# Folding the last 64 channels into a copy of the first 128: two statistics passes instead of three

## The chip, the cores and the metric

One core of one Trainium2 chip. The time is the device time of one execution in microseconds (us); medians of several runs are quoted. All runs here were in the fast state (granted clock 0.989 to 0.994 of full speed in every profiled run). A ratio is the mean time of one kernel's fast runs over that of the other's of the same rounds, so it isn't quite the ratio of the medians beside it.

Engine names in the profile: PE is TensorE's matmul, PEld its weight load, DVE is VectorE, ACT is ScalarE, POOL is GpSimd, SP issues transfers. The names that the lines use most: `st` is the PSUM bank of the statistics, `x` the activations, `sq` their squares, `dev` the variance computed from `st`, `dv` its inverse root spread over partitions by transfers, `yn` the normalised input of the MLP, `ph` and `hid` the MLP's first product and its gelu, `sc` the attention scores, `win` the scaled input of the attention, `vbd` the attention's values, `y` a piece of the convolution. A bank is one of the blocks of PSUM into which TensorE writes its products.

## The reference, cut to what matters

A shifted-window transformer block on 16 images of 192 channels and 56x56 pixels, then a convolution whose weights depend on the image. What the change touches are the two layer norms over the channels:

```python
def _ln(x, g, b, eps=1e-05):
    mu = x.mean(-1, keepdims=True)                  # over 192 channels
    var = ((x - mu) ** 2).mean(-1, keepdims=True)
    return (x - mu) / jnp.sqrt(var + eps) * g + b
h = _ln(transpose(x), norm1_g, norm1_b)             # before the attention
# ... window attention; x1 = shortcut + projection
y = _ln(transpose(x1), norm2_g, norm2_b)            # before the MLP
```

## The kernel before

The work goes in 64 steps of 7 rows of an image in each half (392 pixels a half, `T`). Channels lie on partitions: `x0` holds channels 0 to 127 for both halves, `x1` holds channels 128 to 191, the first half of the image on partitions 0 to 63, the second on 64 to 127. The sums over channels, which cross partitions, are made on TensorE with a constant matrix `sel` of 1/192, 32 columns wide. Each half and each of the two norms ("side") has its own 32 rows of the output, so four such matmuls fill the array side by side.

```python
def norm_squares(key, i, side, engine, ...):
    # squares of x0 and x1 (ACT or GpSimd), then on GpSimd:
    for h in range(2):
        p = slice(h * 64, h * 64 + 64)
        nc.gpsimd.tensor_tensor(s0[p, h], s0[p, h], s1[p], ALU.add)   # line 263
    sqs[key] = s0

def norm_stats(keys, steps):
    for side in keys:
        stats[side] = bank(side)
    for k in range(3):                       # three passes
        for side in keys:
            v0, v1 = flat_of(steps[side])
            for h in range(2):
                p = (side if k < 2 else 1 - side) * 64 + h * 32
                dst = stats[side][p : p + 32, :T]
                if k == 0:   mm(dst, sel[:, 0], v0[:, h], True, False)
                elif k == 1: mm(dst, sel[:, 1 + h], v1, False, True)
                else:        mm(dst, sel[:, 0], sqs[keys[side]][:, h], True, True)
    ...

def norm_vars(keys, tag="dev"):              # mean squared on ACT, then on VectorE:
    ...
    nc.vector.tensor_tensor(d[var[s]], stats[s][var[s], :T], d[var[s]], ALU.subtract)
```

One step of the loop, cut. `A, B_, C, D` are the four pairs of PSUM banks:

```python
for i in range(2, NS + 2):
    A, B_, C, D = pairs
    cs = conv_ready(...)                     # up to two pieces of the convolution
    ...
    norm1_scale(i + 1, dvs.pop(0), nc.vector)
    def after():                             # first tap on ACT, three more on VectorE
        ys.extend(conv_begin(*c) for c in cs[1:])
        for c, y in zip(cs, ys):
            conv_rest(*c, y)
    def between():
        singles[0] = banks(f"st_{i}", C)     # the statistics take bank pair C
        keys.update(stats_of(i))
        if keys:
            var.append(norm_vars(keys))
    mlp_first(i - 2, yns.pop(i - 2), hid, (A, B_, C, D, A, B_), after, between)
    # mlp_first: ph 0..2, gelu 0..2, after(), half of ph 3..5, between(), the rest, gelu 3..5
    top, share = attention_scores(i, *qs.pop(i), (C, D, A, B_))   # first scores: pair C
    # ... softmax, next q/k, spread of 1/sqrt(var) by transfers (dv)
    # ... mlp_wide, yn = x * dv and squares on GpSimd, attention, projection, residual
    pairs = [C, B_, D, A]
```

## Time and profile before

| kernel before | |
|---|---|
| median (first three runs) | 3168.89 us, 3168.42 to 3170.85 |
| PE, DVE, ACT, POOL busy | 99%, 67%, 59%, 31% |
| plain step of the loop | 47.68 us |
| every fourth step (an image's taps are made) | 48.77 us |
| statistics in a step: x passes, sq pass | 1.34 us + 0.77 us |

The busy share says how much of the span an engine executed something. A step is measured from the first statistics matmul to that of the next step, in the list of TensorE's instructions in order of time; since the loop is regular to about 0.01 us in all runs but e6 (a few single steps aside), it is a far finer measure than the total. The lines themselves are in the prediction.

### The profile page before, as it was taken

The page shows a single profiled execution, that of the slowest core. Times are in us where ns is not written, and L with a number is a line of the kernel's source. Part 1 is how long each engine was busy: PE and PEld are TensorE (multiplying, and loading weights), DVE is VectorE, ACT ScalarE, POOL GpSimd, SP SyncE. Part 2 cuts the span into 40 slices and gives each one's busy share as a digit, 9 for nine tenths or more (in the row PEclk, how much of TensorE's full clock was granted, in tenths as well). Part 3 has the DMA queues.
Part 4 walks back from the last instruction along what each step waited for, and adds up shares of the span by engine and source line. Part 5 has one row for each costly group of instructions (what it writes and reads, how often), then busy time and mean ns, then how long its engine had stood idle before and what let it go on. Part 6 is the DMA issues. An engine that isn't in the chain of part 4 may idle for free.

```text
span 3168.7 us, 64205 instructions
## 1 busy us (share of the span) xinstructions
PE 3123.1 (99%) x26162; PEld 1932.8 (61%) x26162; DVE 2126.2 (67%) x3909; ACT 1882.5 (59%) x2990; POOL 975.3 (31%) x882
## 2 busy tenths in 40 slices
PE   8899999999999999999999999999999999999998
PEld 5566566666666666666666666666666666666654
DVE  6645766866766766766767667667667667667664
ACT  3555655656656656556556556556566566566553
POOL 4333233232232332332332332332332332323321
PEclk7999999999999999999999999999999999999999
DMA  4001021111101112011120201211111120111101
GB/s 111 12 21 52 27 63 31 32 57 36 58 27 40 54 32 64 30 52 36 38 57 29 65 26 32 61 32 57 33 43 44 37 62 27 52 39 34 27 27 51
DMA packets 79155, 135.37 MB, mean 43 GB/s; under 512 B 21782, under 2 KB 61468, under 8 KB 76940
## 3 DMA queue, kind: packets, MB, share of 16 engines
q1 hardware_dynamic: 77186, 128.92, 14.0%
q8 instruction: 207, 3.39, 0.5%
q0 software_dynamic: 1168, 1.54, 0.3%
q10 hardware_dynamic: 506, 0.79, 0.1%
q14 instruction: 88, 0.72, 0.1%
HBM read 41.26 MB, written 38.54 MB: 25 GB/s over the span
## 4 chain that ended last, share of the span: by engine, by line
PE 93%; DVE 4%; ACT 3%; issue 0%; DMA 0%; POOL 0%; ACTq 0%; SPq 0%; POOLq 0%; DVEq 0%
PE pf L92 24%; PE ph L92 22%; PE pp L92 8%; PE pv L92 7%; PE po L92 6%; PE pq L92 5%; PE pt L519 5%; PE sc L92 4%; PE st L92 4%; PE pk L92 4%; PE pe L92 4%; DVE vbd L462 1%; DVE x L595 1%; ACT vbd L462 1%; ACT hid L609 0%
## 5 line engine op out<-in xcount | busy, mean ns | idle before, releaser
L92 PE MATMUL ph<-yn,wf 128*128 128x392 f32 (+1 forms) x3072 | 806.2, 499 | 3.8 <-ACT hid L609 3.2
L92 PE MATMUL pf<-hid,wf 128*128 128x392 f32 (+1 forms) x3072 | 802.8, 494 | 3.5 <-ACT hid L609 2.0
L506 POOL TENSOR_TENSOR prob<-e,tot 113x588 f32<-113x588 f32 x256 | 298.2, 1176 | 1189.8 <-DVE tot L505 1168.1
L92 PEld LDWEIGHTS ph<-yn,wf 128*128 128x128 f32 (+1 forms) x3072 | 422.5, 188 | 359.1 <-issue 78.9
L462 ACT COPY vbd<-pv 49x192 f32<-49x192 f32 x512 | 160.5, 314 | 696.2 <-DVE vbd L462 691.6
L92 PEld LDWEIGHTS pf<-hid,wf 128*128 128x128 f32 (+1 forms) x3072 | 386.3, 164 | 303.7 <-issue 120.0
L655 DVE SCALAR_TENSOR_TENSOR x<-pf,cols,x 128x784 f32<-128x784 f32 (+1 forms) x128 | 106.1, 829 | 528.5 <-PE pf L92 485.9
L609 ACT ACTIVATE hid<-ph,f1b 128x784 f32<-128x784 f32 x384 | 337.1, 913 | 100.8 <-PE ph L92 99.4
L263 POOL TENSOR_TENSOR sq<-sq,sq 64x392 f32<-64x392 f32 x252 | 260.4, 1033 | 372.2 <-ACT sq L257 357.9
L718 DVE SCALAR_TENSOR_TENSOR y<-x,wt,y 128x770 f32<-128x770 f32 x282 | 321.1, 1148 | 16.8 <-ACT y L711 8.3
L358 POOL TENSOR_TENSOR yn<-x,dv 128x784 f32<-128x784 f32 x62 | 115.2, 1858 | 534.5 <-DMA dv<-dev 534.5
L92 PEld LDWEIGHTS pv<-wqkv,win 64*128 64x128 f32 (+1 forms) x2048 | 255.7, 189 | 31.5 <-issue 1.2
L92 PE MATMUL pv<-wqkv,win 64*128 64x192 f32 (+1 forms) x2048 | 272.8, 326 | 0.5 <-ACT kbd L416 0.5
L497 DVE TENSOR_TENSOR e<-e,top 113x588 f32<-113x588 f32 x256 | 267.0, 1043 | 8.9
L490 DVE TENSOR_TENSOR e<-sc,bias_t 113x588 f32<-113x588 f32 x256 | 179.4, 763 | 123.8 <-PE sc L92 123.8
L92 PE MATMUL pp<-o,wp 128*128 128x392 f32 (+2 forms) x896 | 251.4, 514 | 0.0
L245 ACT ACT_TABLE_LOAD x193 | 247.6, 1283 | 5.2 <-issue 1.8
L525 ACT COPY prt<-pt 128x678 f32<-128x678 f32 x256 | 179.3, 727 | 116.5 <-PE pt L519 115.1
L500 ACT ACTIVATE e<-e 113x588 f32<-113x588 f32 x256 | 176.8, 691 | 110.0 <-DVE e L497 109.9
L519 PEld LDWEIGHTS pt<-ident,prob 113*128 113x128 f32 x1536 | 166.8, 142 | 72.3 <-issue 39.9
L92 PE MATMUL po<-prt,vbd 128*64 128x49 f32 x6144 | 199.2, 225 | 4.3 <-ACT kbd L416 4.3
L462 DVE COPY vbd<-pv 49x192 f32<-49x192 f32 x512 | 181.2, 354 | 31.9 <-PE pv L92 24.7
(166 smaller groups left out, 3994.8 us busy)
## 6 DMA issues: line engine op xcount, KB each, us to landing
dv<-dev SPq DMA_DIRECT2D x1012, 49.0 KB
x<-in_x_dram SPq DMA_DIRECT2D x15, 1484.0 KB
out_dram<-y SPq DMA_DIRECT2D x48, 392.0 KB
out_dram<-y SPq DMA_DIRECT2D x48, 196.0 KB
x<-in_x_dram SPq DMA_DIRECT2D x16, 392.0 KB
x<-in_x_dram SPq DMA_DIRECT2D x15, 350.0 KB
out_dram<-y SPq DMA_DIRECT2D x16, 308.0 KB
out_dram<-y SPq DMA_DIRECT2D x16, 154.0 KB
```

The costliest lines, as they stand in the source:

```text
L92: nc.tensor.matmul(dst, lhs, rhs, start=start, stop=stop, skip_group_check=True)
L245: nc.scalar.activation(junk, eps_t[0:1], func)
L263: (adder or nc.gpsimd).tensor_tensor(s0[p, h], s0[p, h], s1[p], ALU.add)
L462: copy(dst, src[s * 64 : s * 64 + N, h, :, :, j, :])
L490: nc.vector.tensor_tensor(e, sc[:PW, :, : HEADS * N], rel, ALU.add)
L497: nc.vector.tensor_tensor(ehs[wp], ehs[wp], t.broadcast_to([PW, 2 * HEADS, N]), ALU.subtract)
L500: nc.scalar.activation(es[wp], es[wp], AF.Exp)
L506: nc.gpsimd.tensor_tensor(prob[wp][:PW, :, 0:N], ehs[wp], t.broadcast_to([PW, 2 * HEADS, N]), ALU.mult)
L519: nc.tensor.transpose(pt[:, a, g * PW : (g + 1) * PW], prob[wp][:PW, h : h + 2, :].rearrange("p h k -> p (h k)"), ident[:PW, :PW],)
L525: nc.scalar.copy(prt, pt[:, :, : 3 * PW])
L609: nc.scalar.activation(hid[:, f], phs[f][:, :, :T], AF.Gelu, bias=f1b[:, f : f + 1])
L718: nc.vector.scalar_tensor_tensor(dst, src, wt[:, kc, t : t + 1], dst, ALU.mult, ALU.add)
```

## The change

The intent is to save TensorE a pass. GpSimd, which is idle two thirds of the time, adds the 64 channels of `x1` onto the matching half of `x0`, the result in a new tile `xs`; transfers copy the half that gets nothing added. The matmul over `xs` then gives the whole mean in one pass. To find room for the adds, they and the squares of step i+3 go ahead of `yn` in GpSimd's order.

```diff
+    def norm_sums(key, i, side):
+        v0, v1 = flat_of(i)
+        s0 = one.tile([128, 2, T], F32, tag=("xs", "o")[side], name=f"xs_{key}")
+        nc.sync.dma_start(s0[64:128, 0], v0[64:128, 0])
+        nc.sync.dma_start(s0[0:64, 1], v0[0:64, 1])
+        for h in range(2):
+            p = slice(h * 64, h * 64 + 64)
+            nc.gpsimd.tensor_tensor(s0[p, h], v0[p, h], v1[p], ALU.add)
+        xss[key] = s0
@@ norm_stats
-        for k in range(3):
+        folded = all(k in xss for k in keys.values())
+        for k in (0, 2) if folded else range(3):
...
-                    if k == 0:
+                    if k == 0 and folded:
+                        mm(dst, sel[:, 0], xss[keys[side]][:, h], True, True)
+                    elif k == 0:
@@ the loop (ahead of it the same sums are added for its first steps)
+        if has(i + 3):
+            norm_sums(f"1_{i + 3}", i + 3, 0)
+            norm_squares(f"1_{i + 3}", i + 3, 0, nc.gpsimd)
         if 1 in keys:
             yns[i - 1] = norm2_scale(i - 1, dvs.pop(1), i == NS)
-        if has(i + 3):
-            norm_squares(f"1_{i + 3}", i + 3, 0, nc.gpsimd)
...
             residual(i, pp, pair1, at)
+            norm_sums(f"2_{i}", i, 1)
```

More of the change, by code (lines that the diff above doesn't have):

```diff
@@ L239, in flat_of @@
         return v0.rearrange("p h r c -> p h (r c)"), v1.rearrange("p r c -> p (r c)")
-    sqs, stats = {}, {}
+    sqs, xss, stats = {}, {}, {}
     def table(func):
@@ L284, in norm_stats @@
             sqs.pop(keys[side])
+            xss.pop(keys[side], None)
     def norm_vars(keys, tag="dev"):
@@ L1030, in tile_swin_then_dynamic_conv @@
     attention_v_out(pvs)
+    norm_sums("1_4", 4, 0)
     yns[0] = norm2_scale(0, dvs.pop(1), True)
@@ L1037, in tile_swin_then_dynamic_conv @@
     residual(1, pp, pair1)
+    norm_sums("2_1", 1, 1)
     norm_squares("2_1", 1, 1, nc.scalar)
```

## The prediction

> **What bounds the kernel now.** I read the page first (busy time, slices, chain), then the list of all waits, then one step of the loop in order of time on every engine, then stretches of exactly one step. The page and the chain:
>
> ```profile
> PE 3123.1 (99%) x26162; PEld 1932.8 (61%) x26162; DVE 2126.2 (67%) x3909; ACT 1882.5 (59%) x2990; POOL 975.3 (31%) x882
> PE 93%; DVE 4%; ACT 3%; issue 0%; DMA 0%; POOL 0%; ACTq 0%; SPq 0%; POOLq 0%; DVEq 0%
> ```
>
> TensorE is busy 99% of the span and is 93% of the chain that ended last. "Busy" alone proves little, so I looked at whether TensorE ever waits. In the list of waits no row of PE itself is over 10 us in the whole run, and one step, from the first statistics matmul to the next, takes 47.67 us with TensorE busy for all of it:
>
> ```profile
> 901.17:948.85 47.68, 47.68 (x409) 29.68 (x407) 32.84 (x61) 29.01 (x47) 14.84 (x13) 1.00 0.09 26
> 1140.66:1188.33 47.67, 47.67 (x408) 29.66 (x406) 33.84 (x60) 29.76 (x48) 14.86 (x13) 1.00 0.11 35
> 1236.01:1284.79 48.78, 48.55 (x413) 29.91 (x411) 31.15 (x63) 28.84 (x46) 15.05 (x13) 1.00 0.17 43
> ```
>
> (Columns: length, then busy us of PE, PEld, DVE, ACT, POOL, granted clock, DMA share, GB/s.) The third row is the step after which an image's filter taps are made, one in four; there TensorE gives up 0.23 us to ACT. So a matmul taken out of the loop is worth its slot, as long as nothing else stands within that distance behind it. The statistics slot, in order of time on TensorE:
>
> ```profile
> 1524.26 1.52 PE L92 MATMUL st<-x,sel 128*32 128x392 f32 x16
> 1525.60 0.84 PE L92 MATMUL st<-sq,sel 128*32 128x392 f32 x8
> 1526.37 4.22 PE L92 MATMUL ph<-yn,wf 128*128 128x392 f32 x12
> ```
>
> The 16 instructions on x are two passes (first 128 channels, then last 64) of four logical matmuls, two instructions each; the 8 on sq are the third. Start to start, two passes take 1525.60 - 1524.26 = 1.34 us, so one takes 0.67 us, and the third took 0.77 to the next product.
>
> **What the Trainium skill says.** "TensorE: Matmul & The Clock Gate", Part 3 (the mechanism): matmuls 32 columns wide in different column tiles run at the same time. The trace agrees: eight such instructions take 0.67 us, while twelve of full width take 1526.37 to 1530.52, 0.35 us each. So the removed eight must not be priced at eight times 0.35 (2.8 us a step), and even less at their listed 498 ns. "SBUF — State Buffer", Who interferes with whom: a VectorE instruction with two SBUF inputs contends with a GpSimd one that reads SBUF; one with at most one SBUF input, outside the two-port modes, does not. The trace agrees: a two-input SBUF product of 64x21 elements, median 0.19 us, took up to 1.33 us beside a GpSimd add, while PSUM copies of L462 stay within 338 to 361 ns and residual adds from PSUM (L595) at 604 at most. "DMA: Bandwidth & Descriptors", Latency and other measured facts: a transfer has a fixed cost of about 2 us; here the spreads landed about 2.1 us after issue (below).
>
> **The change part by part.**
>
> *Removed:* the middle pass, in 63 of the loop's steps (60 with both sides, 3 with one; the three statistics rounds before the loop are not folded). The built programs agree: the statistics stand at the same place in TensorE's order, one pass shorter. The estimate is 63 x 0.67 = 42 us. Of the last three steps part is not bound by TensorE, so I count 41 to 42.
>
> *Added on GpSimd:* four adds of 64x392 a step. The same form costs 1033 ns (L263), so 4.1 us a step, 123 x 2 x 1.03 = 254 us in all: POOL goes from 975 to about 1230 us, 39%. Whether they lie on a path depends on where they stand:
>
> ```profile
> 1507.17 1.86 POOL L358 TENSOR_TENSOR yn<-x,dv 128x784 f32<-128x784 f32 x1 [8.46 <-DMA dv<-dev]
> 1508.99 2.10 POOL L362 TENSOR_TENSOR yn<-x,dv 64x392 f32<-64x392 f32 x2
> 1511.16 1.49 POOL L259 TENSOR_TENSOR sq<-x 128x784 f32<-128x784 f32 x1
> 1512.62 0.84 POOL L260 TENSOR_TENSOR sq<-x 128x392 f32<-128x392 f32 x1
> 1513.53 2.10 POOL L263 TENSOR_TENSOR sq<-sq,sq 64x392 f32<-64x392 f32 x2
> 1520.69 2.10 POOL L263 TENSOR_TENSOR sq<-sq,sq 64x392 f32<-64x392 f32 x2 [5.06 <-ACT sq L257]
> ```
>
> The change puts the sums and squares of step i+3 ahead of yn, into the hole of 8.4 us in which GpSimd waits for the spread. The last softmax product ends 1546.38; sums 2.1, squares 1.49 + 0.84 + 2.10 give about 1553.0. The spread lets yn start at 1554.75 in that step, so yn is late by nothing, with 1.7 us left; and yn ends its first part at 1556.6 while its reader, the first ph, starts at 1563.74. This holds only if the adds don't wait for the copies. They don't: the copies fill the half of the partitions that the adds leave alone, and the built program shows the adds waiting for TensorE (the buffer's previous reader) and older transfers, not for their own. The second pair follows the residual: 1515.1 to 1517.2, in the hole before the squares of ACT at 1520.69, which keep their place. VectorE then copies from PSUM, which does not contend; its two-input products start at 1517.97, after it.
>
> *Added transfers:* four a step, 98 KB each, on the SP queue:
>
> ```profile
> 1547.31 10.54 SPq L312 DMA_DIRECT2D dv<-dev  x16
> 1573.70 0.34 SPq L740 DMA_DIRECT2D out_dram<-y  x1
> ```
>
> Sixteen spreads issue in 10.54 us (0.66 each), the eighth at about 1552.6, and its reader starts at 1554.75: 2.1 us to landing. The first two copies go behind the spreads, 1557.9 to 1559.2, landing about 1561; the second two after the residual (1515.1), issued by 1516.5, landing about 1519, with a wide allowance for 98 KB by 1520. The statistics start at 1524.26. Some 24 MB more on 135 MB at 43 GB/s loads nothing. Where an image is loaded, the queue now holds the load back some 5 us until the residual is done; that load took about 6 us and is read about 25 us later.
>
> *Moved:* after the removed pass, everything up to the next step must come 0.67 us earlier. VectorE is the nearest: before it evicts the scores it idles for 1.22 to 2.6 us waiting for TensorE:
>
> ```profile
> 1193.11 1.14 DVE L295 TENSOR_TENSOR dev<-st,dev 64x392 f32<-64x392 f32 x2
> 1195.47 2.80 DVE L490 TENSOR_TENSOR e<-sc,bias_t 113x588 f32<-113x588 f32 x4 [1.22 <-PE sc L92]
> ```
>
> That is the tightest kind of step and leaves 0.55 us. ACT's wait for the statistics is 1.57 us there or more. Before the statistics ACT (third gelu, ends 1524.10) has almost no slack against TensorE (1524.26), but that stretch is not shortened, so no wait forms. The sum: 3168.9 - 42 = 3127 us.
>
> **The rivals.**
> (1) *GpSimd or the copies become the wait:* the adds wait for their transfers after all, and yn stands behind them. Then yn would start around 1567.7 and end its first part near 1569.6, some 6 us after TensorE wants it, 62 times: about +345 us, near 3500. For it: the order sums, squares, yn. Against it: the regions are disjoint and the built program has no such wait.
> (2) *Contention:* GpSimd's sums slow VectorE. If a third of a microsecond a step reached ACT's vbd copies (they follow VectorE's, and end in the gelu with 0.16 us of slack), 0.2 to 0.3 us a step would come back, 15 to 20 us: about 3143. Against it: PSUM readers show no slowing beside GpSimd.
> (3) *The pass was partly hidden:* if the 0.67 us only overlapped other work, TensorE would be no faster: 3165. Against it: PE is busy throughout and the next product follows at once.
> (4) *More waits on TensorE's queue:* the statistics now wait for four transfers as well as GpSimd and ACT. If each cost 0.05 us visibly, 12 us: 3139. Against it: steps whose statistics already wait for loaded images show the same 1.34 us.
>
> **Range and chances.** I hold the plain sum at some 75%; (2) and (4) together some 17%, which sets the upper end; (3) a few per cent; (1) 2%. Below the sum there is little: only one pass per step can go, so 3118 is already three times the uncertainty of the 0.67 us. Predicted 3127 us, range 3119 to 3142. Faster by over 2% would be under 3105.5, that is 63 us from a 42 us removal: 0.02. Slower by 2%: 0.03. Within 2%: 0.95, so a real gain of 1.3% that the 2% line calls the same.
>
> **What would show it.** Right: the steps are 47.0 us long instead of 47.67; 492 fewer statistics instructions on x; the xs matmuls start about 0.67 us ahead of sq; POOL near 1230 us; yn still released by the dv transfer with an idle time near 1.7 us instead of 8.4; VectorE's idle time before the score eviction 0.55 to 1.9 us; PE still 99%. Wrong: PE rows in the list of waits released by POOL yn, POOL xs or DMA xs; L462 or L342 longer; gaps before st or before the first ph.

## The result, and the profile after

The changed kernel takes 3141.32 us (3138.62 to 3141.79, 4 runs) against 3168.65 us of the kernel before beside it: ratio 0.9911, 95% interval 0.9894 to 0.9929. That is inside the range, and 14 us above the point of 3127 us: some 27 of the 42 us came.

The page of the changed kernel, busy times and the chain that ended last:

```profile
PE 3086.4 (98%) x25670; PEld 1931.8 (62%) x25670; DVE 2126.6 (68%) x3909; ACT 1881.5 (60%) x2990; POOL 1219.2 (39%) x1128
PE 84%; DVE 10%; ACT 2%; issue 2%; DMA 1%; POOL 0%; ACTq 0%; SPq 0%; DVEq 0%; POOLq 0%
```

492 TensorE instructions are gone as forecast, and POOL stands at 1219 us (about 1230 were forecast). But TensorE's part of the chain fell from 93 to 84%, and VectorE's rose from 4 to 10%. GpSimd's part is still 0%, so the adds did not become the bound. GpSimd in one step, in order of time, fits the plan:

```profile
1151.11 2.10 POOL L274 TENSOR_TENSOR xs<-x,x 64x392 f32<-64x392 f32 x2
1153.29 1.49 POOL L259 TENSOR_TENSOR sq<-x 128x784 f32<-128x784 f32 x1
1154.74 0.84 POOL L260 TENSOR_TENSOR sq<-x 128x392 f32<-128x392 f32 x1
1155.66 2.09 POOL L263 TENSOR_TENSOR sq<-sq,sq 64x392 f32<-64x392 f32 x2
1159.34 1.85 POOL L373 TENSOR_TENSOR yn<-x,dv 128x784 f32<-128x784 f32 x1 [1.59 <-DMA dv<-dev]
```

The sums and squares run in the hole, and yn still waits for its transfer, 1.59 us in this step, where the prediction had 1.7; over the loop it is 1.4 to 3.6 us, median 2.1 (8 us and more in the last three steps, which have no sums ahead of it).

Four steps in a row, as stretches (length, then busy us of PE, PEld, DVE, ACT, POOL, clock, DMA share, GB/s):

```profile
939.29:986.60 47.31, 47.17 (x400) 29.67 (x399) 33.89 (x60) 29.76 (x48) 18.82 (x17) 1.00 0.15 44
986.60:1034.13 47.53, 47.17 (x400) 29.67 (x398) 34.08 (x61) 29.58 (x47) 18.87 (x17) 1.00 0.26 77
1034.13:1082.32 48.19, 47.96 (x404) 29.88 (x403) 31.18 (x63) 28.82 (x46) 19.01 (x17) 1.00 0.20 51
1082.32:1129.47 47.15, 47.15 (x400) 29.77 (x398) 32.83 (x61) 28.99 (x47) 18.82 (x17) 1.00 0.13 36
```

Forecast were 47.0 us and 48.1 us. The first steps of the loop, which have no convolution yet, are 47.02 us long in this trace; those with it are not. One step of the second kind, TensorE and VectorE in order of time:

```profile
1176.79 0.94 PE L92 MATMUL st<-xs,sel 128*32 128x392 f32 x8
1177.47 0.92 PE L92 MATMUL st<-sq,sel 128*32 128x392 f32 x8
1177.52 4.07 DVE L733 SCALAR_TENSOR_TENSOR y<-x,wt,y 128x770 f32<-128x770 f32 x4
1178.32 4.22 PE L92 MATMUL ph<-yn,wf 128*128 128x392 f32 x12
1181.62 1.14 DVE L310 TENSOR_TENSOR dev<-st,dev 64x392 f32<-64x392 f32 x2
1182.91 2.24 PE L92 MATMUL sc<-kbd,q 64*64 64x98 f32 x96 [0.37 <-DVE dev L310]
```

There is a wait that did not exist before: the score matmuls (sc) start 0.15 us after VectorE's subtraction (dev) ends at 1182.76, and the profile names it. The first scores go to bank pair C, in which the statistics lie, and dev is their last reader. In the kernel before, the like step had dev end at 1193.11 + 1.14 = 1194.25 and the scores start thus (the window of the view ends inside them), behind the same four taps of the convolution:

```profile
1189.02 4.06 DVE L718 SCALAR_TENSOR_TENSOR y<-x,wt,y 128x770 f32<-128x770 f32 x4
1194.59 1.65 PE L92 MATMUL sc<-kbd,q 64*64 64x98 f32 x67
```

So 0.34 us lay between dev and the scores, and the change needed 0.67. Of the 0.34, the 0.15 us that pass between dev's end and a score matmul that waits for it can't be used. Why dev doesn't come earlier with TensorE: from the residual's second set of adds on, the timeline lists no wait of VectorE before dev (waits over 0.15 us are listed). dev starts 15.4 us after these adds start in both kernels (1177.74 to 1193.11, and 1166.19 to 1181.62), while TensorE's way to the scores became a pass shorter. A second, smaller thing: from the first statistics matmul to the next product it takes 1178.32 - 1176.79 = 1.53 us here, where 2.11 - 0.67 = 1.44 follows from the prediction, and 1.59 in the step after the taps; only the early steps have 1.45.

The medians by kind of step (14 rounds of four, from the traces; a: first after the taps, b and c: two pieces of the convolution, d: the taps are made at its end), for all kernels of this study. The ratios are to the kernel before in the same rounds, whose medians were 3168.4 to 3169.8 us. In e6 the b and c steps vary, from 48.2 to 51.4 us:

| kernel | a | b | c | d | time, us | ratio to before |
|---|---|---|---|---|---|---|
| before | 47.68 | 47.68 | 47.68 | 48.77 | 3168.65 | 1 |
| after | 47.15 | 47.31 | 47.53 | 48.19 | 3141.32 | 0.9911 |
| e1 pass dropped, nothing added | 47.02 | 47.24 | 47.46 | 48.11 | 3137.81 | 0.9898 |
| e2 banks exchanged | 47.16 | 47.09 | 47.10 | 48.19 | 3131.91 | 0.9879 |
| e3 sq pass first | 47.02 | 47.30 | 47.53 | 48.11 | 3137.50 | 0.9898 |
| e4 both | 47.02 | 47.02 | 47.02 | 48.11 | 3126.84 | 0.9864 |
| e5 before, banks exchanged | 47.67 | 47.68 | 47.68 | 48.77 | 3168.49 | 0.9998 |
| e6 yn first on GpSimd | 47.34 | 48.72 | 49.06 | 48.59 | 3197.43 | 1.0092 |
| e7 no adds on GpSimd | 47.02 | 47.30 | 47.53 | 48.11 | 3138.71 | 0.9906 |
| e8 all added, three passes kept | 47.68 | 47.68 | 47.68 | 48.77 | 3168.79 | 0.9999 |
| e9 dev earlier on VectorE | 47.15 | 47.10 | 47.10 | 48.19 | 3132.19 | 0.9886 |
| e10 e4 and the taps' products later | 47.02 | 47.02 | 47.02 | 47.46 | 3115.77 | 0.9834 |

Against 47.02 and 48.11 the changed kernel loses 0.13, 0.29, 0.51 and 0.08 us: 1.01 us in four steps, with 14 such rounds about 14 us, which is the missing time (3141.3 against e4's 3126.8).

### The profile page after: what moved, and what is told of

It is laid out like the page before. It is cut to its first block, busy times and chain, and to the rows that moved or that the text cites. A ratio compares the mean times of both kernels' runs of the same rounds, so it can differ in the third digit from the quotient of the medians.

```text
span 3139.3 us, 64443 instructions
## 1 busy us (share of the span) xinstructions
PE 3086.4 (98%) x25670; PEld 1931.8 (62%) x25670; DVE 2126.6 (68%) x3909; ACT 1881.5 (60%) x2990; POOL 1219.2 (39%) x1128
## 4 chain that ended last, share of the span: by engine, by line
PE 84%; DVE 10%; ACT 2%; issue 2%; DMA 1%; POOL 0%; ACTq 0%; SPq 0%; DVEq 0%; POOLq 0%
PE pf L92 24%; PE ph L92 16%; PE pp L92 8%; PE po L92 6%; PE pv L92 5%; PE pq L92 5%; PE pt L534 5%; PE sc L92 4%; PE pk L92 4%; PE pe L92 4%; DVE y L733 3%; PE st L92 2%; DVE vbd L477 2%; DVE x L610 1%; DVE win L357 1%
## 5 line engine op out<-in xcount | busy, mean ns | idle before, releaser
L477 ACT COPY vbd<-pv 49x192 f32<-49x192 f32 x512 | 160.1, 313 | 693.3 <-DVE vbd L477 688.7
L274 POOL TENSOR_TENSOR xs<-x,x 64x392 f32<-64x392 f32 x246 | 248.9, 1012 | 234.9 <-DVE x L610 225.6
```

The lines of the kernel that those rows point to most:

```text
L274: nc.gpsimd.tensor_tensor(s0[p, h], v0[p, h], v1[p], ALU.add)
L477: copy(dst, src[s * 64 : s * 64 + N, h, :, :, j, :])
```

## The experiments

Three theories for the missing 14 us: the removal runs into dev and its PSUM bank (1); the added adds, transfers or waits cost it (2); the waits in TensorE's queue pull the statistics' four column tiles apart (3, a part of 2). A fourth asks whether the new order on GpSimd matters.

### e1: only the removal

```diff
-        for k in range(3):
+        for k in (0, 2) if drop else range(3):      # drop=True in the loop
```

> The kernel before with the middle statistics pass left out of the loop and nothing added (wrong on purpose: the last 64 channels are missing from the mean). Theory 1 (the removal itself runs into VectorE: the score matmuls reuse the PSUM bank of the statistics, which VectorE's subtraction into dev frees, and in the steps with two pieces of the convolution that comes late): most of the missing 14 us is missing here too, about 3138 us (3168.7 - 42 + 12), steps of 47.0, 47.2-47.3, 47.5 and 48.1 us. Theory 2 (the added adds, transfers and waits cost the 14 us): the full gain, about 3127 us, steps of 47.0 throughout and 48.1 in one of four.

Measured 3137.81 us (ratio 0.9898, 0.9882 to 0.9915). The result still passed the comparison, though it is wrong on purpose: the mean enters only as its square in the variance. The kernel adds nothing at all, and steps b and c are still 0.22 and 0.44 us too long, while a and d are at their floor. One of them, in order of time:

```profile
1180.40 1.14 DVE L295 TENSOR_TENSOR dev<-st,dev 64x392 f32<-64x392 f32 x2
1181.68 1.55 PE L92 MATMUL sc<-kbd,q 64*64 64x98 f32 x62 [0.37 <-DVE dev L295]
```

The same wait of 0.37 us stands in a kernel without any of the added work. Theory 1 holds for steps b and c, and the sizes fit: in the kernel before, the medians from dev's end to the first scores are 0.58 us in b and 0.35 in c; less the 0.15 that a waiting score matmul keeps, 0.43 and 0.20 could be given up, and a pass of 0.66 leaves 0.23 and 0.46. What a and d lose in the changed kernel is absent here, so that part belongs to what was added.

### e2: the banks exchanged

```diff
         mlp_first(i - 2, yns.pop(i - 2), hid, (A, B_, C, D, A, B_), after, between)
+        C, D = D, C
```

> The changed kernel with the banks C and D exchanged after the first MLP half, so that the first scores go to a bank that a gelu freed long ago and only the second quarter of the scores needs the statistics' bank, 0.55 us later. Theory 1: the wait for dev goes, 0.22 and 0.43 us in two steps of four, some 9.6 us: about 3131.5 us; what is left above 3127 is the staggered start of the statistics. Theory 2: no change, 3141 us.

Measured 3131.91 us (0.9879, 0.9864 to 0.9894). Steps b and c fall to 47.09 and 47.10 us; a and d stay at 47.16 and 48.19. The wait for dev is gone from the list of waits. In step c the scores now start before dev has ended (1178.88 + 1.14 = 1180.02):

```profile
1178.88 1.14 DVE L310 TENSOR_TENSOR dev<-st,dev 64x392 f32<-64x392 f32 x2
1179.73 2.24 PE L92 MATMUL sc<-kbd,q 64*64 64x98 f32 x96
```

The change costs no instruction: it only gives the first scores a bank that was freed earlier.

### e3 and e4: the sq pass first, and both

```diff
-        for k in (0, 2) if folded else range(3):
+        for k in (2, 0) if folded else range(3):
```

> The changed kernel with the pass over sq put before the pass over xs, so that TensorE's queue works off the waits for the four transfers while sq streams. Theory 3 (the extra waits in TensorE's queue start the four column tiles up to 0.14 us apart in steps where ACT frees the bank last): the statistics slot goes back from 1.53-1.59 us to 1.44-1.45 us in the convolution's steps, but where dev sets the scores nothing is won, so 3 us: about 3138 us. If the stagger has another cause: 3141 us and slots as before.

> Both edits. If theories 1 and 3 together are the whole loss, the plain sum of the prediction is reached: 3126 to 3128 us, steps of 47.02 us and 48.1 us in one of four. If something else holds it, above 3130 us.

e3 measured 3137.50 us (0.9898, 0.9883 to 0.9913): the slot is back at 1.45 us, a and d reach the floor of 47.02 and 48.11, b and c don't move, because there dev is what the scores wait for. e4 measured 3126.84 us (0.9864, 0.9849 to 0.9878), all four kinds of steps at the floor:

```profile
936.28:983.30 47.02, 47.02 (x400) 29.41 (x398) 33.88 (x60) 29.76 (x48) 18.81 (x17) 1.00 0.15 44
983.30:1030.32 47.02, 47.02 (x400) 29.42 (x398) 34.05 (x61) 29.58 (x47) 18.85 (x17) 1.00 0.26 78
1030.32:1078.44 48.12, 47.89 (x405) 29.66 (x403) 31.17 (x63) 28.83 (x46) 19.01 (x17) 1.00 0.21 51
```

How the queue does it can be read from the single records of the changed kernel's trace in a step of kind a (start in us, duration in ns; the first matmul of each of the four tiles and the wait instructions, the weight loads cut):

```
1082.268  51 Tensor EVENT_SEMAPHORE
1082.320 517 TensorMatrix MATMUL  st<-xs
1082.326 517 TensorMatrix MATMUL  st<-xs
1082.375 489 TensorMatrix MATMUL  st<-xs
1082.393  51 Tensor EVENT_SEMAPHORE
1082.500 489 TensorMatrix MATMUL  st<-xs
```

Here a tile whose data come by two semaphores has a wait instruction of 51 ns of its own ahead of it; the one at 1082.393 stands ahead of the last tile, whose weight load waits for GpSimd besides. In the early steps these waits are worked off while TensorE still streams the product before, and the four tiles start within 0.02 us of each other. Where ACT frees the statistics' bank last, the queue stands in front of them, works them off afterwards, and the fourth tile starts 0.18 us after the first (0.12 in steps b, c and d); the next pass inherits the offset, and the slot is 0.08 to 0.14 us longer. With the sq pass first, these wait instructions are gone from between the tiles, and the four tiles start within 0.02 us in all steps (e3, e4). How the queue works the waits off is read from these records; that the order of the passes removes the loss is what e3 shows.

### e5: the exchange without the change

> Control: the kernel before with the banks C and D exchanged in the same way, three passes kept. Theory 1: there dev is done before the scores want the bank (some 0.35 us or more to spare), so nothing changes: 3168 to 3169 us. If the exchange were worth something by itself (about 9 us), 3159 us, and the gain of the exchange in the changed kernel would not show the wait.

Measured 3168.49 us over 12 runs (0.9998, 0.9989 to 1.0007), with steps of the same length to 0.01 us. The exchange gains nothing by itself. Its gain in e2 is the wait.

### e6: GpSimd's old order

```diff
         if 1 in keys:
             yns[i - 1] = norm2_scale(i - 1, dvs.pop(1), i == NS)
+        if has(i + 3):
+            norm_sums(f"1_{i + 3}", i + 3, 0)
+            norm_squares(f"1_{i + 3}", i + 3, 0, nc.gpsimd)
```

> The changed kernel with GpSimd's old order: yn first, then the sums and squares of step i+3. Theory 4 (the sums are free only because they moved into the hole ahead of yn): the second pair of sums then starts about 2.5 us later, beside VectorE's two-input products, which wait for it; dev comes 1 to 2 us later in the steps with two pieces of the convolution, and the scores with it: 3170 to 3200 us. If GpSimd's order doesn't matter: 3141 us.

Measured 3197.43 us (1.0092, 1.0076 to 1.0107): 28 us slower than before, 56 slower than the change. In one step, GpSimd and VectorE in order of time:

```profile
1143.32 2.26 POOL L274 TENSOR_TENSOR xs<-x,x 64x392 f32<-64x392 f32 x2
1143.58 2.37 DVE L349 TENSOR_TENSOR win<-x,dv 128x343 f32<-128x343 f32 x2
1155.83 1.14 DVE L310 TENSOR_TENSOR dev<-st,dev 64x392 f32<-64x392 f32 x2
1157.11 2.24 PE L92 MATMUL sc<-kbd,q 64*64 64x98 f32 x96 [1.30 <-DVE dev L310]
```

and the same two products in the changed kernel, with the PSUM copies ahead of them, which overlap GpSimd's sums (1167.12 to 1169.21):

```profile
1167.52 2.94 DVE L477 COPY vbd<-pv 49x192 f32<-49x192 f32 x8
1170.50 0.95 DVE L349 TENSOR_TENSOR win<-x,dv 128x343 f32<-128x343 f32 x2
```

The products with two SBUF inputs take 2.37 us beside GpSimd's sums and 0.95 us without. The copies from PSUM take 2.94 us in the changed kernel beside the sums, as in the kernel before. The lost time goes on to dev and from there to the scores, whose wait grows to 1.30 us. A part of the loss is another: the statistics slot grows to 1.72 to 1.78 us, with the fourth tile 0.31 to 0.35 us behind the first, which e6 doesn't separate. So the reordering is not decoration: without it the four adds a step cost more than the removed pass gains.

### e7: no adds

```diff
-        nc.sync.dma_start(s0[64:128, 0], v0[64:128, 0])
-        nc.sync.dma_start(s0[0:64, 1], v0[0:64, 1])
-        for h in range(2): ... nc.gpsimd.tensor_tensor(s0[p, h], v0[p, h], v1[p], ALU.add)
+        nc.sync.dma_start(s0[:, 0], v0[:, 0])
+        nc.sync.dma_start(s0[:, 1], v0[:, 1])
```

> The changed kernel without GpSimd's sums: two transfers of 128 partitions copy both halves (wrong on purpose). Prediction and theories 1 and 3: the adds are off the path, 3139 to 3142 us, the same waits for dev. If the adds slow VectorE or hold yn, up to 14 us faster, 3127 us.

Measured 3138.71 us (0.9906, 0.9889 to 0.9922; wrong on purpose, passed the comparison for the reason given at e1). Steps b and c are the changed kernel's; the adds cost VectorE and yn nothing. The one thing that changes, a little below what was expected, is that a and d come to the floor: without the adds the pass over xs waits for GpSimd no more, so its matmuls have one semaphore less, and the slot is back at 1.45 us. That fits theory 3. So the adds are free as work, but the wait for them isn't: it is part of the 0.13 and 0.08 us of steps a and d.

### e8: everything added, nothing removed

```diff
-        folded = all(k in xss for k in keys.values())
+        folded = False
```

> All the added work (sums, transfers, GpSimd's new order), but the statistics read x in three passes as before; xs is made and not read. Prediction: added work alone costs nothing, 3167 to 3171 us. If it costs what the removal lost: about 3183 us.

Measured 3168.79 us over 12 runs (0.9999, 0.999 to 1.0007). 249 us of GpSimd work (246 adds of 1012 ns) and 25 MB of transfers (160.1 MB against 135.4) are hidden completely. This run can't show what waiting for xs costs, since no matmul reads it, nor whether the work would still be hidden in a step a pass shorter; e7 and e4 show the latter.

### e9: dev earlier on VectorE

```diff
     def between():
         ...
             if keys:
                 var.append(norm_vars(keys))        # dev
+            for c, y in zip(cs[1:], ys[1:]):
+                conv_rest(*c, y, (1,))             # last tap and store of the second piece
```

> The changed kernel with VectorE's subtraction into dev moved ahead of the last tap of the second convolution piece (1.02 us earlier on VectorE), banks as they were. Theory 1: the scores no longer wait for dev, as with the exchanged banks, so the same 9.6 us come back: about 3131.5 us, steps of 47.1 us where they were 47.3 and 47.5. If the bank mattered for another reason than dev's lateness: 3141 us.

Measured 3132.19 us (0.9886, 0.987 to 0.9903), the steps of e2 to 0.01 us. The wait goes in either way: by another bank for the scores, or by an earlier dev, the bank's last reader.

### e10: a better kernel

With e4 the three plain steps are TensorE's own length; the fourth is still 1.09 us longer. In the traces VectorE's residual starts there only after the tap products on TensorE (in the kernel before it waits 4.46 us where a plain step has 2.96).

```diff
             def at():                              # called after the residual's first adds
+                taps(b, pooled, pt)
-                convs[-1]["tt"] = taps_hidden(b, pt)
 ...
         residual(i, pp, pair1, at)
+        if pt is not None:
+            convs[-1]["tt"] = taps_hidden(b, pt)
```

> Exchanged banks and sq first, and in the one step of four that makes an image's taps the residual's first adds are written ahead of the tap products, so that they can't wait for those, and the taps' own add goes behind the residual. If the 1.1 us by which that step is longer come from VectorE waiting for the tap products (it starts the residual 1.5 us later there), 15 steps give up to 1.1 us each: 3110 to 3118 us. If not: 3127 us.

Measured 3115.77 us (0.9834, 0.9819 to 0.9848): 1.7% faster than before, the best here. The fourth step falls to 47.46 us. VectorE's residual now waits 2.76 us there instead of 4.46. Of the remaining 0.44 us, the tap products themselves are the larger part: from their start to that of the next product it takes 0.38 us. What makes the rest was not tested. By the measured step lengths, e4 is the prediction's sum and e10 an addition of another kind.

## Why the prediction was right or wrong

- *What bounds the kernel:* right. TensorE sets the time, and a pass taken away is worth 0.66 us a step where nothing follows close (47.02 against 47.68, early steps and e4).
- *The size of the pass:* right. 63 x 0.67 = 42 us gave 3127; e4, which removes both new waits, measured 3126.84.
- *The added adds:* right as work. e8 shows them free, e7 that dropping them doesn't touch steps b and c, and yn still waits for its transfer (1.4 to 3.6 us, 1.7 forecast). TensorE's additional wait for them isn't free (e7, steps a and d): see rival (4).
- *The transfers:* right as far as the trace shows: the list of waits has no wait for a transfer into xs. When they landed isn't in the trace.
- *Rival (1)* did not come; *rival (2)* did not come in the changed kernel, but e6 shows that it would with GpSimd's old order; *rival (3)* is ruled out by e4. *Rival (4)*, more waits on TensorE's queue, came: 0.08 to 0.13 us in steps a and d, and in b and c hidden behind dev (e3). It was put at 12 us and is 3 to 4 us alone (e3: 3141.3 to 3137.5; by the steps 14 x 0.21 = 2.9) and 5 us once dev is out of the way (e2 to e4). The argument against it, steps that already waited for loaded images and kept 1.34 us, failed because those steps are not alike: there, in the kernel before, no wait instruction stands between the tiles of a pass (any stand ahead of the first tile), and the four tiles start within 0.02 us.
- *The step that failed:* "Moved". It took as VectorE's slack its idle time before the score eviction, 1.22 us, "and leaves 0.55 us". That idle time is measured up to the arrival of the scores, but the scores themselves need dev: they reuse the bank that dev reads last. The slack that counts is from dev's end to the scores' start, 1194.25 to 1194.59, 0.34 us, smaller than 0.67, and only 0.20 of it could be used. The idle time that was to fall to 0.55 us stands at 1.00 us in steps b and c of the changed kernel: it didn't shrink as forecast because the scores came late. The two dependencies are in the same loop body (`st_{i}` in C, the first scores in C), so it could have been read before. Of the missing 14 us, 9 to 10 are this term (e2, e9), the rest the queue's.
- *The range* held it because its upper end was made by rivals (2) and (4), of which (4) was real but smaller; the wait that cost most was in none of them. That 3141.3 us lies under 3142 is luck: the cause was another.
- *A misread line and a sum:* the product that "took up to 1.33 us" beside a GpSimd add is one of 64x343 elements (median 0.52 us), whose line mixes three shapes. The products of 64x21 took at most 0.92 us, median 0.18, 45 of 126 of them 0.90 us and more. So GpSimd's adds of the squares held such products up in many steps of the kernel before already, and do in the changed one (44 of 126). Rival (1)'s "+345 us" would be 363 us by its own times (1569.6 - 1563.74, 62 times). Neither bears on the result.

## What to carry to other kernels

When an instruction is taken out of the bounding engine, look at every instruction after it and ask how long ago each thing it needs was done: data, and also the last reader of the buffer that it overwrites. An idle time of another engine is no measure of that, because it may be waiting for the very engine that would wait for it. Here the whole size of the removal was had by exchanging two buffers and the order of two passes, without one more instruction.

## What the Trainium skill lacked or had wrong

- "TensorE: Matmul & The Clock Gate", Part 3 (the mechanism, and the cost of the per-tile semaphore tail): it has tiles starting about 4 ns apart (here about 7 ns where nothing waits between them) and a cost for semaphore increments; it has none for waits between the tiles of one pass. Here a wait of 51 ns between them went with a fourth tile 0.12 to 0.18 us after the first, and the pass pair took 1.53 to 1.59 us instead of 1.45, where another engine freed the bank last.
- "SBUF — State Buffer", Who interferes with whom: its full block of one engine by the other is stated for the two-port modes, and for two SBUF inputs only that they contend, without a size (the slowdowns that it quotes name no instruction). Here two-input products (128x343) took 2.37 us for two beside GpSimd's adds against 0.95 us alone (e6). In the kernel before, the small ones (64x21) waited for the whole add: in all 45 cases in which one started while an add of 1.01 us ran, about 0.14 us into it, it ended 0.04 us after the add and took 0.90 to 0.92 us instead of 0.17. PSUM copies took nothing extra, which agrees with the page.
- "PSUM — Partial Sum Buffer", PSUM bank collisions: it treats two engines on one bank as a matter of correctness that software has to keep apart. The price in time isn't there: with 0.34 us between the end of the last reader of the bank and the next matmul into it, a saving of 0.67 us turned into a wait of 0.37 us, and another bank for the first scores took the wait away (e2).
